# Padded rows for the DRAM tensors and the x tile of layer 0, in a four-layer graph network

## The chip, the cores and the metric

The kernel runs on one core of one Trainium2 chip. The metric is the device time of one execution in microseconds. A core has five engines that run side by side: TensorE (PE, matrix products; its weight loads are listed as PEld), VectorE (DVE), ScalarE (ACT), GpSimd (POOL) and SyncE (SP). Transfers between DRAM and the on-chip memory (SBUF, 128 partitions) are issued by an engine's queue, here nearly all by SP's, and carried out by 16 DMA engines. A transfer consists of runs: stretches of bytes that are contiguous at both ends. The trace records each run as one packet.

## The reference, cut to what matters

The inputs are x (64 graphs, 256 nodes, 256 features) and adj (64 x 256 x 256), all float32. Four layers follow each other, each with a residual and a layer norm. Layer 0 is a recurrence over the 256 nodes, and it is the one that the change is about:

```python
d = jnp.sum(adj, axis=-1)
dinv = jnp.where(d != 0, 1.0 / jnp.where(d != 0, d, 1.0), 0.0)
norm_adjT = jnp.swapaxes(adj, 1, 2) * dinv[:, :, None]

def step(h, i):
    x = jnp.take(h_e, i, axis=1)
    row = jnp.take(norm_adjT, i, axis=1)
    x_par = jnp.einsum('bj,bjd->bd', row, h)          # over all nodes j
    iou = x @ W_ioux.T + b_ioux + x_par @ W_iouh.T + b_iouh
    r, z = jnp.split(iou, 2, axis=1)
    r, z = (jax.nn.sigmoid(r), jax.nn.sigmoid(z))
    hc = jnp.tanh(x @ W_coux.T + b_coux + x_par * r @ W_couh.T + b_couh)
    h_new = z * x_par + (1.0 - z) * hc
    h = jax.lax.dynamic_update_slice(h, h_new[:, None, :], (0, i, 0))
    return (h, None)
```

Node i's step needs the new states of all nodes before it, and the old states (x) of those from i on. Layer 1 is a normalized graph convolution, layer 2 a masked attention with one head, layer 3 a masked attention with eight heads. They work on each graph by itself:

```python
x = _layernorm(x + _L0_gnn_ref(x, adj, ...), axis=-1)
x = _layernorm(x + _L1_gnn_ref(x, adj, ...), axis=-1)
x = _layernorm(x + _L2_gnn_ref(x, adj, ...), axis=-1)
x = _layernorm(x + _L3_gnn_ref(x, adj, ...), axis=-1)
```

## The kernel before, in words

The kernel has a setup, then `_recurrence` (layer 0, all 64 graphs at once, node by node), then `_layers` (layers 1 to 3, a pipeline over graphs). A state of 64 graphs x 256 features lies as 128 partitions x 128 numbers: partition is half of the features times graph.

The sum x_par of a node is put together from parts, by how far back the node j lies:

- From the old states. In the setup, and later beside the steps (`x_side`), PE multiplies adj with x, and `x_out` (L217) stores the products in the DRAM tensor `Us`. `sums_in` (L313) loads the sums of eight nodes at a time as the tile ACC: 128 partitions x 8 nodes x 128 numbers, 512 KB.
- From states long past (`early`). `early_load` (L378) fetches new states from the DRAM tensor `Hd` as the tile Hs (16 to 112 nodes as partitions, eight graphs, 256 features: 8 KB for each partition) and the pieces of adj that go with them as the tile A (runs of 128 bytes). PE multiplies them, and the result is stored in the DRAM tensor `Es` (L430); `early_in_part` (L441) loads it for eight nodes at a time as early_sb, 512 KB.
- From states 9 to some 60 steps back (`late`, L491). They lie in the SBUF ring `Hw`, with the node as the partition. `into_ring` (L652) writes every new state hs into it, in two transfers of 32 KB. PE multiplies ring and adj for the eight nodes of the next block; `send` (L499) stores the result in the DRAM tensor `Lb` and `receive` (L506) loads it back as late_sb, 512 KB. The way through DRAM moves the numbers from one partition layout to the other.
- From the last steps. DVE (`push`, L626) and POOL (`push_far`, L658) add the newest states to ACC directly.

`flush` (L634) copies 32 rows of the ring to `Hd` every 32 steps, in transfers of 8, 16 or 32 partitions with 32 KB each. `load_x` (L564) loads x of eight nodes in two transfers of 256 KB (tile xq). Every tile is transferred by SP's queue.

The order is written out by hand in the loop over n (L757). A block is eight steps, and p = n mod 8. In the steps p < 4, at most two waiting loads a step are issued (`next_load`: Hs, A, S, raw, the x side). The end of a step issues early_sb at p = 0, ACC at p = 1 and xq at p = 2. The states go into the ring at p > 3, two a step. The late products run at p = 0 to 3, their results leave with Lb and come back with late_sb around p = 4 and 5, and POOL adds late_sb to ACC (L876) at p = 6 and 7. At every 32nd step, the tables S, raw and rows of the next 32 nodes are loaded too. All of this goes through one queue in program order, so a transfer that has to wait there holds up all those behind it.

The tiles in DRAM are dense: node, graph and feature lie behind each other. So where a load takes several nodes of one partition, its run is as long as all of them: 4096 bytes for ACC, early_sb and late_sb (8 nodes x 512 bytes), 4096 for xq (4 nodes x 1024), 8192 for Hs (8 graphs x 1024) and 32,768 for the flush (32 graphs x 1024).

Of the kernel before, what the change touches and what calls it, by code (L numbers as in the profile page):

```python
# [9 lines left out]
F32 = mybir.dt.float32  # L10
# [9 lines left out]
P = 128  # L20
# [50 lines left out]
def _recurrence(tc, ident, Hd, x, adj, W_ioux, b_ioux, W_iouh, b_iouh, W_coux, b_coux, W_couh, b_couh, wide, then):  # L71
# [19 lines left out]
    nc = tc.nc  # L91
    B, N, D = x.shape
    T = 32
    NB = N // T
    U = 8
# [4 lines left out]
    NG = B // 4  # L100
# [3 lines left out]
    with ExitStack() as ctx:  # L104
# [85 lines left out]
        for w in range(2):  # L190
            first = (w * T - W + T // 2) % W
# [13 lines left out]
        )  # L205

        dram = ctx.enter_context(tc.tile_pool(name="r_dram", bufs=2, space=bass.MemoryType.DRAM))
        Us = dram.tile([2, B, N, P], F32, name="Us", bufs=1)

        def x_product(pb, at, A, Xs):  # L210

# [42 lines left out]
        def copy_later(out, in_, then=None):  # L254
            def f(n):
                nc.scalar.copy(out, in_)
                held.pop(0)
                if then:
                    then(n)

            copies.append(f)

        def load_later(out, in_, rank):

            begun = []

            def f(n):
                with nc.allow_non_contiguous_dma(reason="bias vector across partitions"):
                    nc.sync.dma_start(out, in_)
                begun.append(n)  # L270

            loads.append((rank, f))
            loads.sort(key=lambda e: e[0])
            return begun
# [5 lines left out]
        def at_step(n, f):  # L280
            transfers.setdefault(n, []).append(f)
# [3 lines left out]
        def base_bank(shape, name):  # L285

            while len(held) == 3:
                next_of(copies, now)
            held.append(name)
            return ps.tile(shape, F32, tag="base", name=name, bufs=3)  # L290
# [85 lines left out]
        Es = {}  # L376

        def early_load(e, got=[]):  # L378

            _, k, lo, hi, t = early.pop(e)  # L380
            rows = hi - lo
            if t == 0:
                Es[k, lo] = dram.tile([2, NG, 4, T, P], F32, name=f"Es_{k}_{lo}", bufs=1)
            Hs = wide.tile([P, GB, D], F32, tag="wide", name=f"Hs_{k}_{lo}_{t}")
            last = [load_later(
                Hs[0:rows], Hd[lo:hi, t * GB:(t + 1) * GB, :], 1
            )]
            if t % 2 == 0:
                A = stream.tile([P, 2 * GB, T], F32, tag="A", name=f"A_{k}_{lo}_{t}")
                last.append(load_later(  # L390
                    A[0:rows],
                    adj[t * GB:(t + 2) * GB, lo:hi, k * T:(k + 1) * T].rearrange("b j i -> j b i"), 1
                ))
                got[:] = [A]
            early_in.append((last, k, lo, hi, t, Hs, *got))

        def early_ahead(n):
            ready = [e for e, piece in enumerate(early) if piece[0] <= n]
            if len(early_in) < 4 and ready:

                half = [e for e in ready if early[e][4] % 2 and early[e - 1:e] != [
                    early[e][0:4] + (early[e][4] - 1,)
                ]]
                early_load((half + ready)[0])
# [86 lines left out]
        def late(first):  # L491

            k, i = divmod(first, T)
            An = tables[k]["An"]
            lb = stream.tile([P, NG, D], F32, tag="lb", name=f"lb_{first}", bufs=1)
            Lb = dram.tile([2, NG, 4, U, P], F32, tag="Lb", name=f"Lb_{first}")
            sides[first] = blk.tile([P, U, P], F32, tag="late", name=f"late_sb_{first}", bufs=1)

            def send():  # L499
                for c in range(2):  # L500
                    nc.sync.dma_start(
                        Lb[c].rearrange("n q u f -> (q u) n f"),
                        lb[i // U::T // U, :, c * P:(c + 1) * P],
                    )

            def receive():  # L506
                nc.sync.dma_start(sides[first], Lb.rearrange("c n q u f -> (c n q) u f"))

            def then(n):
                at_step(n, send)  # L510
                at_step(n + 1, receive)

            n = yield
            for u in range(0, NG // 2, 2):
                pb = [base_bank([P, 2, D], f"late_{first}_{u}_{g}") for g in range(2)]
                for e in range(2):
                    for q in range(4):
                        for g in range(2):
                            rows = slice(g * W, (g + 1) * W)
                            b = (u + e) * 4 + q  # L520
                            nc.tensor.matmul(  # L521
                                pb[g][q * T:(q + 1) * T, e, :],
                                An[rows, b].rearrange("p u s -> p (u s)"),
                                Hw[rows, b, :], start=True, stop=True,
                            )
                    if e:
                        for g in range(2):
                            at = g * NG // 2 + u
                            copy_later(
                                lb[:, at:at + 2, :], pb[g],  # L530
                                then if g and u + 2 == NG // 2 else None,
                            )
                    n = yield
# [29 lines left out]

        def load_x(a):  # L564

            xq = stream.tile([P, U // 2, D], F32, tag="xq", name=f"xq_{a}")
            for h in range(2):
                at = a * U + h * U // 2
                nc.sync.dma_start(xq[h * B:(h + 1) * B], x[:, at:at + U // 2, :])
            return xq  # L570

        def flip_x(a, e, xq):
# [138 lines left out]
        stream = ctx.enter_context(tc.tile_pool(name="r_stream", bufs=2))  # L711
# [3 lines left out]
        tables[0]["Sd"] = chain_S(0)  # L715
        tables[0]["An"] = late_load(0)
        xq = {a: load_x(a) for a in range(2)}
        for a in range(3):
            sums_in(a)
# [37 lines left out]
        for now in range(N):  # L757
            n = now
            k, i = divmod(n, T)
# [24 lines left out]
            if p == 0 and U < n + U < N:  # L784
                late_side = late(n + U)
                next(late_side)
# [98 lines left out]
            if p == 2 and n // U + 2 < N // U:  # L885
                xq[n // U + 2] = load_x(n // U + 2)
# [404 lines left out]
def _load_layers(nc, wide, load, w1, b1, l2, l3):  # L1291

    t1, t2, t3 = (wide.tile([P, 8, 256], F32, tag="wide", name=f"weights_{l}") for l in (1, 2, 3))
    nat = t1[:, 0:2]
    load(nat, w1.rearrange("(c p) d -> p c d", p=P))
    W = []
    for t, l in ((t2, l2), (t3, l3)):
        W.append({})  # L1300
        for s, n in enumerate("qkvo"):
            W[-1][n] = t[:, 2 * s:2 * s + 2]
            load(W[-1][n], l["W" + n].rearrange("(k p) n -> p k n", p=P))
    rows = [t1[:, 2 + s] for s in range(3)]
    for r, b in zip(rows, (b1, l2["bo"], l3["bo"])):
        load(r, b.unsqueeze(0).to_broadcast([P, 256]))
    cols = t1[:, 5, 0:12].rearrange("p (s c) -> p s c", c=2)
    for s, b in enumerate((l2["bq"], l2["bk"], l3["bq"], l3["bk"], l3["bv"], l2["bv"])):
        load(cols[:, s, :], b.rearrange("(c p) -> p c", p=P))
    return nat, *W, *rows, cols  # L1310
# [111 lines left out]
@with_exitstack  # L1422
def kernel(ctx: ExitStack, tc: tile.TileContext, ins, out):
    nc = tc.nc
    x, adj = ins["x"], ins["adj"]
    B, N, D = x.shape
    main = ctx.enter_context(tc.tile_pool(name="main", bufs=1))
    dram = ctx.enter_context(tc.tile_pool(name="dram", bufs=1, space=bass.MemoryType.DRAM))
    ident = main.tile([P, P], F32, name="ident")
    make_identity(nc, ident)  # L1430
    Hd = dram.tile([N, B, D], F32, name="Hd")
    l2, l3 = (
        {w + n: ins[f"{l}_gnn_{w}{n}"] for w in "Wb" for n in "vkqo"} for l in ("L2", "L3")
    )
    wide = ctx.enter_context(tc.tile_pool(name="wide", bufs=4))
    weights = []

    def load_layers(load):
        weights.extend(
            _load_layers(nc, wide, load, ins["L1_gnn_W"], ins["L1_gnn_b"], l2, l3)  # L1440
        )

    _recurrence(
        tc, ident, Hd, x, adj,
        *(ins["L0_gnn_" + n] for n in (
            "W_ioux", "b_ioux", "W_iouh", "b_iouh", "W_coux", "b_coux", "W_couh", "b_couh"
        )),
        wide, load_layers,
    )
    Yd = dram.tile([B, P, 2, D], F32, name="Yd")  # L1450
    found = _layers(tc, ident, Hd, Yd, x, adj, weights, out)
    with tc.If(found > 0):
        _layer_3(tc, ident, Yd, adj, l3, out)
# [36 lines left out]
```

## Time and profile before

| What | Before |
|---|---|
| median of 3 runs | 3354.61 us (3352.26 to 3360.83) |
| profiled execution, time and span | 3353.51 us, 3351.7 us |
| mean granted clock of PE | 0.976 |
| PE, DVE, ACT, POOL busy | 3131.6, 2554.5, 1838.6, 1845.0 us |
| DMA packets, bytes | 528,608, 364.62 MB |
| packets on SP's queue | 510,520 |
| setup, before the first step | 138 us |
| recurrence, 256 steps | 138 to 1472 us |
| layers 1 to 3 | from about 1480 us to the end |

The rows come from the page of the profile, the last three from the trace's start times. A page's busy share is a mean over stages that are limited by different things, so the stages have to be read apart: the slices of the page and the windows (busy time of each engine in a stretch, followed by the granted clock, the busy share of the DMA engines and the GB/s that they moved) do that. The list of waits gives, for an engine and a line, what ended its idle time, with the total in us, the number of times and the longest. The chain of waits is the chain of work that ended last, as start, length, and what it was. In a timeline, SPq is SP's queue issuing a transfer; its duration is the time for which the queue was held by the issue, and not that of the transfer.

### The profile page before, as it was taken

To read this page: it belongs to the slowest core of one execution; us is meant where nothing else is said; L and a number is where in the kernel's file an instruction comes from. 1 tells how busy PE (TensorE), PEld (TensorE's weight loads), DVE (VectorE), ACT (ScalarE), POOL (GpSimd) and SP (SyncE) were. 2 spreads that over 40 slices of the span, in tenths; PEclk is the share of its full clock that TensorE was granted. 3 is DMA by queue.
4 is the path that set the end of the run, shared out by engine and by line. 5 is a ranking of instruction groups with operands and counts; after the bars stand their busy time and mean duration, and the time that the engine had idled before them with its cause. 6 is when DMAs were issued, how large, how long until landed. Compare 5 with 4: busy or idle time off the path is not lost.

```text
span 3351.7 us, 78940 instructions
## 1 busy us (share of the span) xinstructions
PE 3131.6 (93%) x28584; PEld 2311.5 (69%) x28584; DVE 2554.5 (76%) x7381; ACT 1838.6 (55%) x4754; POOL 1845.0 (55%) x2165
## 2 busy tenths in 40 slices
PE   5799998998879998969999999999999999999997
PEld 4566665555545555547888888888888888888885
DVE  3487777776667878856888888888888888888885
ACT  0155554544445544535666666666666666666664
POOL 2377777766667878833444444444444444444443
PEclk7899999999999999989999999999999999999999
DMA  9856685788877675241221211122222222222210
GB/s 292 247 161 156 168 194 152 179 198 207 204 181 178 163 174 152 65 105 47 56 57 54 57 56 54 54 55 58 57 58 58 58 57 58 57 58 58 58 33 20
DMA packets 528608, 364.62 MB, mean 109 GB/s; under 512 B 246620, under 2 KB 494568, under 8 KB 522984
## 3 DMA queue, kind: packets, MB, share of 16 engines
q1 hardware_dynamic: 510520, 342.63, 39.6%
q10 hardware_dynamic: 17696, 16.91, 1.5%
q8 instruction: 229, 3.75, 0.5%
q14 instruction: 163, 1.34, 0.1%
HBM read 240.78 MB, written 99.61 MB: 102 GB/s over the span
## 4 chain that ended last, share of the span: by engine, by line
PE 77%; DMA 8%; DVE 7%; issue 2%; SPq 2%; ACT 2%; POOL 1%; DVEq 0%; ACTq 0%; POOLq 0%
PE mm L997 14%; PE rc L605 6%; PE rc L597 4%; PE s L1195 4%; PE mm_2f L997 3%; PE mm_3v L997 3%; PE mm_3f L997 3%; PE mm_2v L997 3%; PE late L521 3%; PE mm_t L997 3%; PE mm_2s L997 3%; PE mm_g L997 3%; PE mm_2w L997 3%; PE o L1230 3%; DVE ACC L630 3%; PE o L1221 3%
## 5 line engine op out<-in xcount | busy, mean ns | idle before, releaser
L1207 POOL TENSOR_TENSOR p3s<-p 128x256 f32<-128x256 f32 x512 | 358.9, 733 | 364.7 <-ACT p L1205 364.6
L630 DVE SCALAR_TENSOR_TENSOR ACC<-keep,S,ACC 128x128 f32<-128x128 f32 x1712 | 479.1, 343 | 16.9 <-POOL ACC L876 11.2
L997 PE MATMUL mm<-xT,weights 128*128 128x256 f32 x2048 | 483.7, 384 | 2.7 <-ACT xT L1094 2.7
L997 PEld LDWEIGHTS mm<-xT,weights 128*128 128x128 f32 x2048 | 386.0, 191 | 79.9 <-issue 25.5
L1204 DVE TENSOR_TENSOR p<-s,neg 128x512 f32<-128x512 f32 x512 | 317.6, 682 | 118.2 <-PE s L1195 118.2
L667 POOL TENSOR_TENSOR ACC<-ACC,far 128x384 f32<-128x384 f32 (+1 forms) x313 | 372.1, 1189 | 24.5
L663 POOL TENSOR_TENSOR far<-hs,S 128x384 f32<-128x384 f32 (+1 forms) x313 | 304.7, 973 | 4.7
L1205 ACT ACTIVATE p<-p 128x512 f32<-128x512 f32 x512 | 292.4, 626 | 1.6 <-DVE p L1204 1.6
L961 ACT ACTIVATE y<-y,shift,rstd 128x256 f32<-128x256 f32 x512 | 272.9, 599 | 26.6 <-DVE shift L959 22.7
L597 PE MATMUL rc<-WxT,xqT 128*64 128x256 f32 x2048 | 274.8, 390 | 1.1 <-issue 1.1
L1119 ACT ACTIVATE qk<-mm,weights 128x256 f32<-128x256 f32 x256 | 107.5, 471 | 301.9 <-PE mm L997 301.9
L805 POOL TENSOR_TENSOR ready<-ACC,dinv 128x128 f32<-128x128 f32 x255 | 102.1, 400 | 304.7 <-DVE ACC L630 304.2
L1108 POOL TENSOR_TENSOR y<-y,g 128x512 f32<-128x512 f32 x64 | 81.0, 1266 | 301.8 <-issue 301.8
L1244 DVE RECIPROCAL rT<-o 128x256 f32<-128x256 f32 x128 | 223.7, 1748 | 0.3 <-PE o L1221 0.2
L949 DVE BATCH_NORM_STATS2 st<-y 128x6 f32<-128x256 f32 x512 | 209.6, 409 | 13.1 <-POOL y L1108 10.3
L521 PE MATMUL late<-Hw,An 64*32 64x256 f32 x3840 | 166.7, 400 | 42.1 <-DMA Hw<-hs 18.8
L605 PE MATMUL rc<-WhT,rT 128*64 128x128 f32 x2048 | 172.5, 290 | 35.6 <-DVE rT L828 33.2
L824 ACT ACTIVATE rs<-rc 128x128 f32<-128x128 f32 x256 | 71.1, 278 | 245.0 <-PE rc L605 245.0
L605 PEld LDWEIGHTS rc<-WhT,rT 128*64 128x64 f32 x2048 | 109.1, 138 | 133.2 <-DVE rT L828 110.8
L953 POOL TENSOR_TENSOR rstd<-rstd,mhalf 128x2 f32<-128x2 f32 x256 | 173.8, 697 | 47.9 <-DVE rstd L952 34.6
L1066 POOL TENSOR_TENSOR dis<-dis,mhalf 128x2 f32<-128x2 f32 x64 | 44.9, 702 | 273.2 <-DVE dis L1065 261.8
L605 PE MATMUL rc<-WhT,xpT 128*64 128x128 f32 x2048 | 169.4, 286 | 18.1 <-ACT xpT L614 18.1
(162 smaller groups left out, 7255.4 us busy)
## 6 DMA issues: line engine op xcount, KB each, us to landing
xX<-in_x_dram ACTq DMA_DIRECT2D x16, 1024.0 KB
Us<-xu SPq DMA_DIRECT2D x64, 256.0 KB
xq<-in_x_dram SPq DMA_DIRECT2D x64, 256.0 KB
ACC<-Us SPq DMA_DIRECT2D x32, 512.0 KB
Es<-eu SPq DMA_DIRECT2D x64, 256.0 KB
early_sb<-Es SPq DMA_DIRECT2D x32, 512.0 KB
xin<-in_x_dram SPq DMA_DIRECT2D x64, 256.0 KB
ad<-in_adj_dram SPq DMA_DIRECT2D x64, 256.0 KB
```

The costliest lines, as they stand in the source:

```text
L521: nc.tensor.matmul(pb[g][q * T:(q + 1) * T, e, :], An[rows, b].rearrange("p u s -> p (u s)"), Hw[rows, b, :], start=True, stop=True,)
L597: nc.tensor.matmul(G[o * B:(o + 1) * B], xqT[a, i // 2][:, i % 2, kc, h * B:(h + 1) * B], WxT[:, kc, o, gates], start=False, stop=False, s ...
L605: nc.tensor.matmul(G[o * B:(o + 1) * B], hT[:, kc * B:(kc + 1) * B], WhT[:, kc, o, g], start=False, stop=(kc == 1), skip_group_check=True,)
L630: nc.vector.scalar_tensor_tensor(acc[:, 0, :], keep[:, j % 2, :], s, acc[:, 0, :], ALU.mult, ALU.add)
L663: nc.gpsimd.tensor_mul(tmp[:, 0:count, :], hs.unsqueeze(1).to_broadcast(shape), s.unsqueeze(2).to_broadcast(shape),)
L667: nc.gpsimd.tensor_add(acc, acc, tmp[:, 0:count, :])
L961: nc.scalar.activation(y[:, c, :], y[:, c, :], AF.Identity, bias=shift[:, c:c + 1], scale=rstd[:, c:c + 1],)
L997: nc.tensor.matmul(pm[:, c, :], lhsT[:, k, c * P:(c + 1) * P], rhs[:, k, :], start=(k == 0), stop=(k == 1),)
L1204: nc.vector.tensor_add(p, s_ps[i], self.neg3)
L1205: nc.scalar.activation(p, p, AF.Exp, scale=ISQ)
L1207: nc.gpsimd.tensor_add(both, p[:, 0, :], p[:, 1, :])
L1244: nc.vector.reciprocal(rT, o_ps[:, 1, :])
```

## The change

Five DRAM tensors or groups of them and one SBUF tile get longer rows, of which only the first part is used. `Us`, every `Es` and every `Lb` get rows of 128 + 64 numbers, of which 128 are used; `Hd` gets rows of 256 + 64; the SBUF tile xq gets 256 + 4. Every instruction and every transfer is the same as before in number, order and bytes. But a load over several rows is no longer contiguous at both ends, so it goes in runs of one row: 512 bytes for ACC, early_sb and late_sb, 1024 bytes for Hs, for the flush and for xq.

```diff
-        Us = dram.tile([2, B, N, P], F32, name="Us", bufs=1)
+        Us = dram.tile([2, B, N, P + 64], F32, name="Us", bufs=1)[..., 0:P]
...
-                Es[k, lo] = dram.tile([2, NG, 4, T, P], F32, name=f"Es_{k}_{lo}", bufs=1)
+                Es[k, lo] = dram.tile(
+                [2, NG, 4, T, P + 64], F32, name=f"Es_{k}_{lo}", bufs=1
+            )[..., 0:P]
...
-            Lb = dram.tile([2, NG, 4, U, P], F32, tag="Lb", name=f"Lb_{first}")
+            Lb = dram.tile([2, NG, 4, U, P + 64], F32, tag="Lb", name=f"Lb_{first}")[..., 0:P]
...
-            xq = stream.tile([P, U // 2, D], F32, tag="xq", name=f"xq_{a}")
+            xq = stream.tile([P, U // 2, D + 4], F32, tag="xq", name=f"xq_{a}")
...
-                nc.sync.dma_start(xq[h * B:(h + 1) * B], x[:, at:at + U // 2, :])
+                nc.sync.dma_start(xq[h * B:(h + 1) * B, :, 0:D], x[:, at:at + U // 2, :])
...
-    Hd = dram.tile([N, B, D], F32, name="Hd")
+    Hd = dram.tile([N, B, D + 64], F32, name="Hd")[:, :, 0:D]
```

## The prediction

> **What bounds the kernel now.** I read the page's slices first, then the chain of waits, the list of waits, SP's timeline and the windows. The slices show two halves:
>
> ```profile
> DMA  9856685788877675241221211122222222222210
> GB/s 292 247 161 156 168 194 152 179 198 207 204 181 178 163 174 152 65 105 47 56 57 54 57 56 54 54 55 58 57 58 58 58 57 58 57 58 58 58 33 20
> DMA packets 528608, 364.62 MB, mean 109 GB/s; under 512 B 246620, under 2 KB 494568, under 8 KB 522984
> ```
>
> From slice 18 on (1480 us) the layers run with the DMA engines 20% busy and PE busy for 1830 of 1860 us. Of the padded tensors only y<-Hd is read there, and that load already goes in runs of 1024 bytes, since one graph's rows lie apart. I count those 1880 us as untouched. What can move is the recurrence, 138 to 1472 us. The start times of the product rT (L828) put its 256 steps at 5.2 us on average, and eight calm steps at 37.5 to 40.5 us. The blocks of eight that begin at 499, 665, 755, 800, 847, 942 and 993 us take 47.7, 49.9, 45.4, 47.4, 53.4, 51.3 and 48.4. That is some 65 us over calm in seven blocks, and the chain of waits names DMA in them:
>
> ```profile
> 786.37 7.92 DMA Lb<-lb
> ...
> 798.64 4.17 DMA Hw<-hs
> ...
> 803.91 5.43 DMA Hw<-hs
> 809.69 0.67 PE late L521 x16
> ...
> 841.28 3.78 DMA late_sb<-Lb
> ```
>
> The reader should see the order: a store of the sides to DRAM that lands late, copies of the state queued behind its read-back, then PE's late products waiting. The list of waits agrees:
>
> ```profile
> PE late L521 <- DMA Hw<-hs: 18.8, 7, 5.6
> POOL ACC L876 <- DMA late_sb<-Lb: 13.7, 4, 6.2
> PE late L521 <- DMA Hs<-Hd: 5.5, 2, 4.7
> ```
>
> These transfers are late because one queue, SP's, carries everything in order. Its timeline in such a block:
>
> ```profile
> 804.71 0.60 SPq L269 DMA_DIRECT2D Hs<-Hd  x1
> 805.40 0.37 SPq L269 DMA_DIRECT2D A<-in_adj_dram  x1
> 805.87 6.21 SPq L430 DMA_DIRECT2D Es<-eu  x2
> 812.12 1.31 SPq L447 DMA_DIRECT2D early_sb<-Es  x1
> ...
> 816.93 11.55 SPq L269 DMA_DIRECT2D Hs<-Hd  x1
> ...
> 831.16 5.75 SPq L269 DMA_DIRECT2D raw<-in_adj_dram  x1
> 837.01 1.31 SPq L501 DMA_DIRECT2D Lb<-lb  x2
> ```
>
> An issue normally takes 0.3 to 0.7 us. These long ones stand where too much is still in the queue. By the trace's issue and packet records, two things stop SP:[...] about 2000 runs in flight (the two Es of 512 runs each stand behind A with 1792 runs of 128 bytes; raw stands behind S with 2624). So the number of runs matters by itself, and the change raises it.
>
> [...] The rows[...] (busy time by engine, then clock, DMA share, GB/s):
>
> ```profile
> 849.00:850.00 1.00, 1.00 (x14) 0.75 (x11) 0.90 (x4) 0.40 (x1) 0.92 (x2) 1.00 1.13 340
> 137.00:139.00 2.00, 1.91 (x16) 1.31 (x13) 0.42 (x1) 0.11 (x1) 2.00 (x3) 0.61 1.02 418
> 819.00:825.00 6.00, 5.89 (x97) 3.30 (x93) 5.51 (x19) 3.43 (x11) 2.68 (x3) 1.00 1.00 253
> 649.00:651.00 2.00, 2.00 (x33) 1.15 (x25) 1.97 (x9) 0.94 (x5) 1.07 (x2) 1.00 1.02 169
> 653.00:655.00 2.00, 2.00 (x27) 1.13 (x23) 1.93 (x9) 0.27 (x1) 1.80 (x3) 1.00 0.57 87
> ```
>
> Row one is Es and Hw in 512-byte runs, row two ACC in 4096-byte runs over 128 partitions, row three mostly Hs in 8192-byte runs over 112 partitions, row four mostly xq in 4096-byte runs over 64. [...]418 against 340 for the run length, and 169 for 64 partitions although the runs are long. The packet records say the same: a 32 KB run of Hd<-Hw takes 2.0 us at the median with 32 rows, 2.7 with 16 and 4.7 with 8; an 8 KB run of Hs takes 0.50 with 112 rows and 0.61 with 64. I go by both: what makes Hs slow is mostly the partitions, which the change leaves alone.
>
> **The change, part by part.** Bytes stay at 364.62 MB. Stores to Us, Es and Lb and the last Hd<-hs have 512-byte rows already: nothing. What is cut:
>
> 1. ACC<-Us (32), early_sb<-Es (32), late_sb<-Lb (30): 128 runs of 4096 bytes become 1024 of 512. 524 KB at 418 GB/s is 1.25 us, at 340 it is 1.54: +0.3 each, 28 us of DMA time in all. A trace reason for less: when several loads overlap, the 4096-byte runs take 0.22 us on average and not the 0.16 of a calm one, so part is lost today already (bound 0).
> 2. Hs<-Hd (64 transfers, 4608 runs of 8192 bytes become 36,864 of 1024). A 1024-byte packet over 128 partitions takes 0.046 us in the records, so 356 GB/s over 16 engines. The 112-row load, 917 KB, is 3.6 us at 253 and 2.6 at 356: at best -1.0. For 64 rows and fewer[...] 0. I take a third of the best for the 32 loads of 112 and 80 rows, -0.4 each, -12 us of DMA time. Bounds: 0, and -42 if every Hs (37.7 MB) went at 356.
> 3. Hd<-Hw (24; 496 runs of 32 KB become 15,872 of 1024) and xq (64; 64 runs of 4096 become 256 of 1024, its rows now at a pitch of 1040 bytes):[...] 0. Bounds -10 and +10 us of DMA time.
> 4. The queue. Packets grow by 84,224 + 32,256 + 15,376 + 12,288 = 144,144. Hs of 112 rows, with 112 runs today, fits beside A's 1792 under the 2000; with 896 it does not, nor does ACC's 1024 beside A's 1280, nor two loads of 1024 beside each other. The next one is then let in only when the one ahead is done, and the engines run dry between. What that costs is seen between S and raw, 653 to 655 us: a share of 0.57 over 2 us, 0.86 us idle. With 32 A loads and a hundred loads of 896 or 1024 runs I count about 24 such gaps in the busy blocks (300 to 1000 us): +21 us of idle DMA. Bounds: 0, if more is admitted than I think, and 100, if each of some 110 pairs pays.
>
> What of this reaches the end? Between 300 and 1000 us the DMA share is 0.7 to 0.8, and about half of its blocks (7 of some 17) show a stall that ends on DMA; where they do not, the next p<4 stage absorbs the delay. I take half for what falls there. Part 1: two thirds of 28 falls in these blocks, half is +9. Part 2: half of -12 is -6. Part 4: half of +21 is +10. Sum +13 us. Before 138 us the setup is DMA-bound, but its stores and loads are not cut; the first ACC load, which DVE waits for 12.5 us, is 0.3 longer. I neglect it. The cover for the rest is PE, DVE and POOL work of the steps; were it gone everywhere, parts 1, 2 and 4 would cost 37 us.
>
> The sum stands against the profiled run's own 3353.5 us (span 3351.7): 3366.5. The median of the runs is 1.1 above that run, so 3367.
>
> **Rivals.**
>
> Faster: short runs flow better. If Hs goes at 356 GB/s and the flush gains too, the backlog ahead of Lb (three Hs of 896 KB stand there at 816 us) lands 3 us sooner, in about eight blocks: -24, so 3331. For it: 253 GB/s at a DMA share of 1.00 is far below 418[...]. Against it: xq is slow too with runs half as long, and follows the row count. It decides once Hs falls by over 0.8 us a load with fewer gaps than 10.
>
> Hidden: the DMA work changes by a few us a block and the steps cover it, 3355. For it: blocks 21 to 31 (after 1040 us) have a share of 0.4 to 0.67 and, but for the one that begins at 1199 us, no stall to speak of. Against it: seven blocks have no slack.
>
> Much slower: every pair of 1024-run loads pays a gap, SP is held longer, and Lb, late_sb and the copies of hs, which follow in the same queue, are late in 12 to 15 blocks by 4 to 5 us: +60, 3415. Against it: loads of 512 and 1024 runs kept the DMA share at 0.96 before 138 us, though ACT's queue helped there.
>
> No effect: the runs are merged anyway and packets stay at 528,608: 3355.
>
> **How the numbers follow.** A run of this kernel can't tell less than 0.3%, 10 us, from no change (its three runs span 8.6). Chances: forecast (+10 to +40) 0.40, faster 0.26, hidden 0.20, much slower 0.10, no effect 0.04. So slower 0.50, same 0.24, faster 0.26. The range leaves out the far half of the faster case and the upper half of the much slower one: 3332 to 3405. The forecast's own range is 3364 to 3394.
>
> **What would show it.** Right: about 672,750 packets and the same bytes; a window with ACC loads alone at 340 GB/s and not 418; Hs of 64 rows as slow as now; more time in SP's issues of A, ACC and Hs; longer blocks among those named, and the layers at the same length. Wrong: Hs windows at 320 GB/s or more, a shorter Lb or Hw<-hs on the chain, or stalls of SP that shrink because fewer bytes stand in the queue.

## The result, and the profile after

The changed kernel takes 3386.78 us (median of 4 runs, 3385.11 to 3392.17), the kernel before 3353.44 beside it: a ratio of 1.0099, with a 95% interval of 1.0079 to 1.0118, so +33 us where +13 was forecast. The page of the changed kernel, its span, the slices of the DMA engines, the packets and SP's queue (packets, MB, share of 16 engines' span):

```profile
span 3383.4 us, 78940 instructions
...
DMA  9856686788787575331222222222222222222210
...
DMA packets 672752, 364.62 MB, mean 108 GB/s; under 512 B 246620, under 2 KB 659944, under 8 KB 672232
...
q1 hardware_dynamic: 654664, 342.63, 41.0%
```

The bytes are the same and there are 144,144 packets more, as counted ahead. The starts of rT, from its first to its last, give the stages: setup +0.7 us, recurrence from 1330.6 to 1361.0, +30.4, and all that follows from 1879.9 to 1880.6. So nearly all of the loss lies in the recurrence. The list of waits names who is late (total in us, times, longest), here for 140 to 1480 us; the line numbers are two higher than before, as the change adds two lines:

```profile
POOL ACC L878 <- DMA late_sb<-Lb: 34.8, 9, 6.9
...
PE late L523 <- DMA Hw<-hs: 22.7, 7, 4.9
...
POOL An L481 <- DMA raw<-in_adj_dram: 16.0, 2, 9.7
...
PE late L523 <- DMA A<-in_adj_dram: 9.4, 2, 5.6
```

POOL waited 13.7 us in 4 places for late_sb before, and now 34.8 in 9. The chain of waits (start, length) shows the same order as before, in more blocks: the side's store, its read-back, then a copy of the state.

```profile
666.07 3.65 DMA Lb<-lb
669.80 5.21 DMA late_sb<-Lb
...
681.04 5.08 DMA Hw<-hs
...
802.05 6.88 DMA Lb<-lb
...
809.06 4.15 DMA late_sb<-Lb
...
819.17 5.37 DMA Hw<-hs
...
1004.96 6.93 DMA Lb<-lb
...
1011.96 4.31 DMA late_sb<-Lb
```

In the recurrence, late_sb stands on that chain 8 times with 35.7 us, against 3 times with 10.2 before.

The run length shows where the forecast looked for it. This is the window with ACC loads alone:

```profile
137.00:139.00 2.00, 1.65 (x12) 0.90 (x8) 0.38 (x1) 0.00 (x0) 1.49 (x3) 0.50 1.15 347
```

347 GB/s in 512-byte runs, where 4096-byte runs had 418. So the mechanism of part 1 is there; the experiments ask what the rest of the 33 us is.

### The profile page after: what moved, and what is told of

Its sections match the earlier page's. It is cut to its first block, busy times and chain, and to the rows that moved or that the text cites. A ratio compares the mean times of both kernels' runs of the same rounds, so it can differ in the third digit from the quotient of the medians.

```text
span 3383.4 us, 78940 instructions
## 1 busy us (share of the span) xinstructions
PE 3138.8 (93%) x28584; PEld 2316.1 (68%) x28584; DVE 2553.4 (75%) x7381; ACT 1838.8 (54%) x4754; POOL 1842.8 (54%) x2165
## 3 DMA queue, kind: packets, MB, share of 16 engines
q8 instruction: 229, 3.75, 0.5%
## 4 chain that ended last, share of the span: by engine, by line
PE 76%; DMA 8%; DVE 8%; issue 2%; ACT 2%; SPq 2%; POOL 1%; DVEq 0%; POOLq 0%; ACTq 0%
PE mm L999 14%; PE rc L607 6%; PE rc L599 4%; PE s L1197 4%; PE mm_2f L999 3%; PE mm_3v L999 3%; DVE ACC L632 3%; PE late L523 3%; PE mm_3f L999 3%; PE mm_2v L999 3%; PE mm_t L999 3%; PE mm_2s L999 3%; PE mm_g L999 3%; PE mm_2w L999 3%; PE o L1232 3%; PE o L1223 2%
## 5 line engine op out<-in xcount | busy, mean ns | idle before, releaser
L951 DVE BATCH_NORM_STATS2 st<-y 128x6 f32<-128x256 f32 x512 | 209.6, 409 | 13.0 <-POOL y L1110 10.2
```

## Experiments

All times below are differences to the kernel before, run in the same set on the same chip, and worked out as (ratio - 1) x 3355 us. Single changes of 4 to 7 us are close to what the intervals (about 4 us either way) can tell.

### Which part costs: one edit at a time

The rates come first. A stretch behind the last layer was added to the kernel before: some 235 us of loads of x and adj into tiles of their own, with nothing else running. Nothing was left out.

```diff
+            (long,) * 6, (short,) * 6, (hs_long,) * 4, (hs_short,) * 4,
+            (few_long,) * 4, (few_short,) * 4,
+            (hs_long, cut) * 3, (hs_short, cut) * 3, (long, cut) * 3, (short, cut) * 3,
```

Here long and short are 512 KB over 128 partitions in runs of 4096 and 512 bytes; hs is 112 partitions in runs of 8192 and 1024; few is the same with 64; cut is a load in 128-byte runs like A's, 1792 of them.

> The kernel before, with loads added behind the last layer, when nothing else uses the DMA engines: six loads of 512 KB to 128 partitions in runs of 4096 bytes, six in runs of 512; four of 112 rows of 8 KB in one run each and four in runs of 1024; the same with 64 rows; and alternating pairs with a load of 1792 runs of 128 bytes. The added time itself says nothing. Run-length theory (part 1 of the forecast): about 415 GB/s for the 4096-byte runs, 340 for the 512-byte ones. [...]the 64-row loads pace alike with both run lengths, near 200 GB/s; the 112-row loads differ by under 10%. Its rival: the 112-row loads reach 330 GB/s or more in runs of 1024 and stay under 280 in runs of 8192. Queue theory (part 4): a load of 896 or 1024 runs in front of one of 1792 leaves the engines idle for about 0.9 us between them, a load of 112 or 128 runs leaves no gap. If neither pair shows a gap, part 4 falls.

Windows in the steady part of each group, in the order long, short, hs_long, hs_short, few_long, few_short, hs_long with cut, hs_short with cut (the last three numbers are clock, DMA share and GB/s):

```profile
3470.00:3473.00 3.00, 0.00 (x0) 0.00 (x0) 0.29 (x2) 0.00 (x0) 0.00 (x0) 0.50 1.02 400
3479.00:3484.00 5.00, 0.00 (x0) 0.00 (x0) 0.58 (x4) 0.00 (x0) 0.00 (x0) 0.50 1.20 290
3490.00:3497.00 7.00, 0.00 (x0) 0.00 (x0) 0.44 (x3) 0.00 (x0) 0.00 (x0) 0.50 1.00 286
3503.00:3510.00 7.00, 0.00 (x0) 0.00 (x0) 0.29 (x2) 0.00 (x0) 0.00 (x0) 0.50 1.11 284
3516.00:3521.00 5.00, 0.00 (x0) 0.00 (x0) 0.29 (x2) 0.00 (x0) 0.00 (x0) 0.50 1.02 210
3527.00:3532.00 5.00, 0.00 (x0) 0.00 (x0) 0.29 (x2) 0.00 (x0) 0.00 (x0) 0.50 1.13 205
3534.00:3546.00 12.00, 0.00 (x0) 0.00 (x0) 0.73 (x5) 0.00 (x0) 0.00 (x0) 0.50 1.05 244
3547.00:3561.00 14.00, 0.00 (x0) 0.00 (x0) 0.88 (x6) 0.00 (x0) 0.00 (x0) 0.50 1.07 236
```

Three readings. Runs of 512 bytes back to back drop to 290 GB/s. The pattern of Hs gains nothing from short runs, with 112 partitions (286 and 284) or with 64 (210 and 205), where the forecast had -0.4 us a load for 80 and 112. And the pair with A's runs keeps the DMA share at 1.07: the gap of 0.86 us that part 4 took from the stretch between S and raw is not there, but for one dip of about half a microsecond (a share of 0.85 over 3550 to 3553 us), at the first pair of the row, which SP issued after a wait. The pairs of 512-byte runs with A's, not shown, have a share of 0.93 over 3570 to 3581 us; it is 0.36 from 3573.5 to 3575.5, again where SP had waited, and 1.12 from there to 3581. So a gap at every pair is not seen.

Then the change was taken apart. Each of these kernels has some lines of the change and leaves the others as before: only Lb; only Hd; only Us and Es; the whole again; the x tile alone; and the four DRAM edits without the x tile.

```diff
+            Lb = dram.tile([2, NG, 4, U, P + 64], F32, tag="Lb", name=f"Lb_{first}")[..., 0:P]
...
+    Hd = dram.tile([N, B, D + 64], F32, name="Hd")[:, :, 0:D]
...
+        Us = dram.tile([2, B, N, P + 64], F32, name="Us", bufs=1)[..., 0:P]
```

> Only the sides Lb have padded rows, so that only the 30 loads late_sb<-Lb go in runs of 512 bytes. My forecast's sum gives this part a third of part 1 and little of part 4: +3 to +5 us. The rival that the trace after suggests (POOL's wait for late_sb grew from 13.7 us in 4 waits to 34.8 in 9): this read-back has no slack, because POOL waits for it at p = 6 and 7 and the copies of the state stand behind it in the queue: +12 to +20 us, more than half of the whole loss.

> Only the states Hd have padded rows: Hs loads and the flush in runs of 1024 bytes. Queue theory: A with up to 1792 runs can no longer share the queue with Hs, +8 to +15 us. Faster-flow rival: Hs and flush land sooner, -5 to -15 us. Read-back rival: within 4 us of before.

> Only Us and Es have padded rows: the 64 loads of ACC and early_sb in runs of 512 bytes. Forecast: two thirds of part 1 and the pairs with A and with each other of part 4, +8 to +12 us. Read-back rival: these loads are issued 8 to 16 steps ahead of their use, so 0 to +4 us.

> The changed kernel once more, beside the kernels below on one chip. The three parts run alone lost 6.4, 7.0 and 4.4 us by their ratios, 18 in sum. If the parts add up and xq costs nothing, this is +18; if they don't (each takes the slack that another would need) or if xq costs, it is +28 to +36, as when it was first measured.

> Only the tile xq is padded, to a pitch of 1040 bytes. Forecast (part 3): 0, within 3 us. Rival: a pitch[...] makes each run slower (its packets rose from 73 ns a KB to 84), +5 to +15 us.

> The changed kernel with the tile xq dense as before. If xq costs nothing, the same as the changed kernel; if the pitch of 1040 bytes is what was overlooked, 8 to 15 us less; it is +18 if the three other parts simply add.

| Kernel | Ratio, 95% interval | us |
|---|---|---|
| only Lb: late_sb in 512 | 1.0019, 1.0008 to 1.0031 | +6.4 |
| only Us and Es: ACC and early_sb in 512 | 1.0013, 1.0002 to 1.0024 | +4.4 |
| only Hd: Hs and the flush in 1024 | 1.0021, 1.0012 to 1.0031 | +7.0 |
| these three together | 1.0044, 1.0027 to 1.0060 | +14.8 |
| only the x tile's rows | 1.0045, 1.0029 to 1.0062 | +15.1 |
| the whole change again | 1.0079, 1.0063 to 1.0096 | +26.5 |

The parts add up, within their intervals: the three DRAM parts to 17.8 where 14.8 was measured, and 14.8 and 15.1 to 29.9 where the whole has 26.5 here and 33 in the first set. But the x tile, taken as free, costs as much as the other three together. A second stretch of added loads asks whether its rate is the reason: x over twice 64 partitions, at a pitch of 1024, 1040 and 1280 bytes, and 128 partitions in runs of 4096, 2048, 1024 and 512.

```diff
+                (runs_4096,) * 6, (runs_2048,) * 6, (runs_1024,) * 6, (runs_512,) * 6,
+                (half(D),) * 6, (half(D + 4),) * 6, (half(D + 64),) * 6,
```

> The kernel before with loads added behind the last layer: 512 KB to 128 partitions in runs of 4096, 2048, 1024 and 512 bytes, six each; the xq pattern (two halves of 64 partitions) with a pitch of 1024, 1040 and 1280 bytes; and single loads of 512 KB with runs of 4096 and of 512 bytes, each waited for. Run-length theory: about 400, 380, 345 and 290 GB/s (the first and the last as the first series gave them). Alignment theory: the xq pattern is 10% or more slower at 1040 than at 1280[...]. A single load takes 0.5 to 0.8 us longer from issue to use in runs of 512.

It measured 394, 358, 362 and 290 GB/s for the four run lengths over 128 partitions, and 393 for 2048 bytes, 339 for 1024 and 290 for 512 in a second turn, so that only the shortest runs stand clearly apart in both. A single load that is waited for takes 3.25 to 3.47 us from its issue to VectorE's use of it in runs of 4096 bytes and 3.56 to 3.75 in runs of 512: 0.3 longer, as the forecast had it, and not 0.5 to 0.8. The windows of the x pattern, with dense rows, rows at 1040 and rows at 1280 bytes:

```profile
3399.00:3405.00 6.00, 0.00 (x0) 0.00 (x0) 0.37 (x3) 0.00 (x0) 0.00 (x0) 0.50 1.03 235
3412.00:3422.00 10.00, 0.00 (x0) 0.00 (x0) 0.61 (x4) 0.00 (x0) 0.00 (x0) 0.50 1.13 222
3427.00:3434.00 7.00, 0.00 (x0) 0.00 (x0) 0.46 (x3) 0.00 (x0) 0.00 (x0) 0.50 1.12 235
```

235, 222 and 235 GB/s; a second turn of the same loads gave 248, 229 and 232. Six per cent on 64 loads of 1.1 us (256 KB at 235 GB/s) is an estimated 4 us of DMA time, and not 15 us of the kernel's. That speaks against the rate but does not exclude it: inside the kernel the padded x tile's packets take 11 to 14 us more in sum.

### Runs, or places? The x tile without its short runs

The tile xq lies in a pool of SBUF (the stream pool) together with other tiles. Padding it also moves what lies behind it. Two kernels separate that: dense x tiles with 64 bytes behind each (runs as before, neighbours moved by as much as in the change), and two runs of 2048 bytes with 32 bytes between them. The padded x tile was run again with them.

```diff
-            xq = stream.tile([P, U // 2, D], F32, tag="xq", name=f"xq_{a}")
+            xq = stream.tile([P, U // 2 * D + 16], F32, tag="xq", name=f"xq_{a}")[:, 0:U // 2 * D].rearrange("p (u d) -> p u d", d=D)
```

> The x tile's rows at 1040 bytes alone, a second time and beside the two that follow. If its first measurement (+15 us) is a property of the edit, +15 within 6. If it came from that set of executions, whose spread was some 10 us either way, 0 to +5.

> The kernel before with 64 bytes of padding behind each x tile: its rows stay dense, the transfers stay in runs of 4096 bytes, only what lies behind the tile in on-chip memory moves by as much as with the padded rows. Theory of addresses (what costs is that the other tiles moved): +15, like the padded rows. Theory of runs (what costs is the 256 runs in place of 64 in each transfer): 0 within 4. Theory of a kernel so finely timed that any edit disturbs it: anywhere from +4 to +15.

> Each partition's x rows in two runs of 2048 bytes with 32 bytes between, so 128 runs a transfer in place of 64 (and not 256). The loads behind the last layer gave 2048-byte runs about the rate of longer ones. If the number of runs in SP's queue is what costs, a third of what the padded rows cost (+5 within 4, since 64 runs more in place of 192 more); if the padding itself or its odd addresses cost, +15; if only runs of 1024 bytes are slow, 0.

Padded again: 1.0047 (1.0030 to 1.0065), +15.8. Dense with 64 bytes behind: 1.0032 (1.0018 to 1.0047), +10.7. Two runs of 2048: 1.0041 (1.0025 to 1.0057), +13.8. The theory of runs falls: a kernel whose packets are those of the kernel before, to the last one, has most of the loss.

That could still mean that any edit hurts so finely timed a kernel, or that kernels compared in this way come out slower for no reason of their own. Four more: an unchanged copy; one more instruction in the setup; the DRAM tensors as large as in the change but with dense rows, so that only addresses in DRAM move; and 32 bytes behind the dense x tile in place of 64.

```diff
+    nc.vector.tensor_copy(ident[0:1, 0:1], ident[0:1, 0:1])
...
-    Hd = dram.tile([N, B, D], F32, name="Hd")
+    Hd = dram.tile([N * B * (D + 64)], F32, name="Hd")[0:N * B * D].rearrange("(n b d) -> n b d", n=N, b=B)
...
+            xq = stream.tile([P, U // 2 * D + 8], F32, tag="xq", name=f"xq_{a}")[:, 0:U // 2 * D].rearrange("p (u d) -> p u d", d=D)
```

> The kernel before, unchanged. If the intervals mean what they say: a ratio of 1.000 within 0.0015 (0 within 5 us). If kernels that are compared with the kernel before come out slower for a reason that is not in them, +4 to +10 us, and each single part must be read against that.

> The kernel before with one more instruction in the setup: VectorE copies one number of ident onto itself. No address and no transfer changes. Theory of a finely timed kernel that any edit disturbs: +4 to +12. Theories of runs and of addresses: 0 within 4.

> Us, Es, Lb and Hd allocated as large as in the changed kernel, but their rows dense, so runs and queue are those of the kernel before and only addresses in DRAM move. The three DRAM parts together cost +15 with their shorter runs. Theory of runs (94 loads that take 0.5 us longer back to back, half of it on the path): 0 within 4. Theory of addresses: +8 to +15. Theory of any edit: +4 to +12.

> Dense x tiles with 32 bytes behind each in place of 64. Theory of addresses on the chip: +5 to +14 (64 bytes moved it by some 11, and two runs of 2048 bytes with 32 bytes between by 14). Theory of runs: 0 within 4. Theory of any edit: +4 to +12.

| Kernel | Ratio, 95% interval | us |
|---|---|---|
| unchanged copy | 0.9997, 0.9985 to 1.0009 | -1 |
| one more instruction | 0.9998, 0.9986 to 1.0010 | -1 |
| larger DRAM tensors, rows dense | 0.9997, 0.9986 to 1.0009 | -1 |
| 32 bytes behind each x tile | 1.0054, 1.0035 to 1.0072 | +18 |

So the comparison is sound, and neither an edit as such nor these addresses in DRAM cost anything that can be measured: what the three DRAM parts cost is their run length. On the chip it is the other way round: where the neighbours lie costs 11 to 18 us.

### The same x tile, moved out of the way

If that is so, the padded x tile is free where it moves nobody. It was put into a pool of its own, opened behind the two others, so that the tiles behind x in them lie 8192 bytes lower and keep their places modulo 8192: dense, padded, and with the whole change.

```diff
+        last_pool = ctx.enter_context(tc.tile_pool(name="r_last", bufs=2))
...
+            xq = last_pool.tile([P, U // 2, D + 4], F32, tag="xq", name=f"xq_{a}")
```

> The kernel before with the x tile in a pool of its own, opened last, so that the other tiles of the two pools lie 8192 bytes lower and keep their places modulo 8192. Control for the next run. If only the odd 32 or 64 bytes matter: 0 within 5. If any move of the tiles costs: +10 to +18.

> The same with the x tile's rows at 1040 bytes: its transfers go in runs of 1024 bytes, and no other tile moves against the control. If the move of the other tiles was the whole cost of the padded x rows: the control's ratio within 4 us. If the runs cost: the control's +8 to +15.

> The whole change, with its x tile in that last pool. If what is left is the three DRAM parts: +15 within 5, as they cost together. If the runs of the x tile cost too: +26 to +33, as the change as it stands.

Dense 0.9990 (0.9981 to 1.0000), padded 0.9990 (0.9977 to 1.0002), the whole change 1.0051 (1.0036 to 1.0065), +17. The padded x tile, runs of 1024 bytes and all, costs nothing there, although its packets do take longer: their times, summed over a run and spread over 16 engines, are 73.0 us dense and 86.1 padded. Its own second buffer moves by 64 bytes there too, so it is the neighbours that count. The whole change without the moved neighbours costs what its DRAM parts cost, within the intervals: +17 against the kernel before and some +20 against the dense control, which is the fairer measure, as the setup is shorter in the traces of these three kernels (133.8 to 138.7 us, against 139.7 to 141.2 in the kernel before and the three that match it). None of them is clearly faster than the kernel before.

### What a moved neighbour does, in one place

The first place where the traces part is the end of the second block of eight steps. SP sends late_sb, two rows loads and then twelve copies of the state to the ring. First the unchanged copy, in SP's timeline (start, time for which SP is held):

```profile
199.41 0.38 SPq L507 DMA_DIRECT2D late_sb<-Lb  x1
199.90 1.18 SPq L301 DMA_DIRECT2D rows<-in_adj_dram  x2
201.12 11.02 SPq L656 DMA_DIRECT2D Hw<-hs  x12
212.25 0.93 SPq L220 DMA_DIRECT2D Us<-xu  x2
```

The window over the six microseconds in which these transfers run, in the copy:

```profile
200.00:206.00 6.00, 6.00 (x64) 4.46 (x61) 4.73 (x18) 3.06 (x10) 5.70 (x6) 1.00 0.69 189
```

And the list of waits of the copy from 200 to 222 us, where it names the stores and what follows them:

```profile
ACT xu L256 <- DMA Us<-xu: 1.6, 1, 1.6
...
PE rc L605 <- ACT xpT L614: 1.2, 1, 1.2
```

PE's first products behind that wait (in brackets, its length and what ended it), and the window around them:

```profile
217.81 0.66 PE L605 MATMUL rc<-WhT,xpT 128*64 128x128 f32 x8 [1.25 <-ACT xpT L614]
...
217.50:220.90 3.40, 3.00 (x53) 1.93 (x57) 1.50 (x6) 2.00 (x9) 3.17 (x4) 1.00 1.12 349
```

Now the kernel with 64 bytes behind the dense x tile. It is here 1.7 us earlier than the copy, because its setup was that much shorter. SP's timeline:

```profile
197.67 0.40 SPq L507 DMA_DIRECT2D late_sb<-Lb  x1
198.16 1.18 SPq L301 DMA_DIRECT2D rows<-in_adj_dram  x2
199.39 12.40 SPq L656 DMA_DIRECT2D Hw<-hs  x12
211.90 1.38 SPq L220 DMA_DIRECT2D Us<-xu  x2
```

The same window of it, counted from the same step:

```profile
198.30:204.30 6.00, 6.00 (x64) 4.46 (x61) 4.73 (x18) 3.06 (x10) 5.63 (x6) 1.00 0.79 187
```

And its list of waits, from 198 to 222 us:

```profile
ACT xu L256 <- DMA Us<-xu: 3.4, 1, 3.4
...
PE rc L605 <- ACT xpT L614: 3.1, 1, 3.1
```

The same products in it, and their window:

```profile
217.87 1.12 PE L605 MATMUL rc<-WhT,xpT 128*64 128x128 f32 x8 [3.06 <-ACT xpT L614]
...
217.50:220.90 3.40, 3.03 (x33) 1.98 (x33) 0.51 (x3) 1.89 (x8) 2.00 (x2) 0.50 1.13 358
```

About the same bytes (189 and 187 GB/s over 6 us) take the DMA engines 0.79 of the time and not 0.69; a 4096-byte packet there takes 275 ns on average and not 237. So the ring's copies hold SP 1.4 us longer, the stores to Us that follow are late, ACT, which wants to overwrite xu, waits 1.8 us longer, and PE behind it 1.8 (3.06 and not 1.25).

The step is 2.8 us longer, and the last microsecond has another source. After the wait of 3.06 us, PE's clock is granted at 0.50 for 3.4 us, and the same eight products take 1.12 us and not 0.66; after the wait of 1.25 us the clock stays at 1.00. So a stall costs more here than it lasts. Over the whole recurrence the clock stands at 0.50 for 58 to 72 us in the kernel before and the three that match it, for 85 and 99 in the two traces of the changed kernel, and for 61 to 89 in the five with only the x tile edited. The eight products took 1.7 times as long at 0.50. Were it twice for all of PE's work there, half of the 13 to 41 us that the changed kernel spends more at 0.50 would be lost: at most 7 to 20 us of its loss, an estimate from these sums. It follows the waits and is not their cause: at 200 to 206 us both kernels have 1.00.

The engines themselves are not slower. The two traces have the same 78,940 instructions with the same semaphores, and the medians of VectorE's, ScalarE's and GpSimd's lines in the recurrence differ by at most 3 ns.

The place is not a single execution's accident: in the five kernels in which only the x tile is edited in place the share in these 6 us is 0.78 to 0.81 and the step loses 1.3 to 2.8 us; in the kernel before, the one with one more instruction, the one with larger DRAM tensors and the two with the x tile in its own pool, the share is 0.67 to 0.71 and the step differs by -0.03 to +0.5 us. The share alone doesn't make the loss, though: the three DRAM parts together have 0.78 there, with late_sb in 512-byte runs, and this step loses 0.05. Nor does the step need moved tiles to lose: Hd alone has a share of 0.66 and loses 1.1. What happens in the other blocks was not followed step by step.

Why a packet takes longer is not shown. When x is edited in place, the tiles behind it in the stream pool stand 64 or 128 bytes from their old places, and 8192 bytes from them when x has its own pool; no other move was tried. What the records of packets give is uneven:

- In this stretch a 4096-byte packet takes 16% longer (275 and 237 ns), although half of these packets belong to late_sb, which lies in another pool and did not move.
- Stores from the moved tiles xu, eu and lb do take longer, but by little: the 512-byte packets of Us<-xu average 29.2 to 29.5 ns in the five kernels with x edited in place, against 27.9 to 28.1 with the old places. Es<-eu has 29.2 to 29.9 against 28.0 to 28.6, and Lb<-lb 28.7 to 29.1 against 27.7 to 28.0, but 27.7 with 32 bytes behind x.
- The source hs of the ring's copies moves too, and its packets stay nearly as they were: 28.2 to 28.5 ns where the tiles moved by 128 bytes, against 27.9 to 28.4.

The DMA time as a whole says little: up to 1490 us, SP's packets sum to 957 to 970 us in the four kernels with the old runs and places, and to 967 to 976 in the three with moved neighbours and x in runs of 2048 bytes or more.

## Why the prediction was wrong, and where it was right

Direction and the stage were right: slower, in the recurrence alone, through late_sb, the ring's copies and SP. The size was too small by 20 us. The step that failed most is part 3's zero for xq: it was priced by its 64 partitions alone, and the padded tile costs 15 us, because it moves the tiles behind it. The second is part 2: Hs and the flush in short runs were to save 6 us, and cost 7. Part 1 was 2 us too low, and part 4's +10 has no ground that was found. Together, 13 + 15 + 13 + 2 - 10 is 33.

Step by step, with the packet times of each tile summed over the run and spread over 16 engines (packets counted to transfers in the order of issue), four kernels with the runs of before (the kernel itself, the copy, the one with one more instruction, the larger DRAM tensors) against the changed one:

| Tile | Before, us | After, us |
|---|---|---|
| ACC | 54.8 to 56.3 | 68.0 |
| early_sb | 55.3 to 57.4 | 60.0 |
| late_sb | 46.3 to 50.0 | 57.2 |
| Hs and flush together | 231.4 to 233.8 | 247.4 |
| xq | 74.1 to 75.8 | 85.8 |

- Part 1, run length of ACC, early_sb, late_sb: right. +28 us of DMA time was forecast and about +25 came (12, 4 and 9). Half of what falls in the busy blocks on the path, +9: the parts alone gave 4.4 + 6.4 = 10.8. The 290 GB/s of loads back to back, against 400, would have given 0.5 us a load, an estimate, but among the recurrence's other traffic ACC and late_sb pay 0.3 to 0.4, and early_sb 0.1.
- Part 2, Hs: wrong in sign. -12 us of DMA time and -6 on the path were forecast; the packets of Hs and flush take about +15 and the part alone costs +7. "I take a third of the best" for 80 and 112 rows was the failing step: alone, the pattern has one rate at both run lengths, and in the recurrence it is slower with the short one; why, is open. The window of 253 GB/s was not its long runs: with nothing else running 286 and 284 GB/s stand alike. There the rate of long runs went with the partitions: 210 GB/s with 64, 286 with 112, 394 and 400 with 128.
- Part 3, flush and xq, "0": right for the flush to the eye (it can't be told from Hs), and right for xq's runs, whose +11 to +14 us of DMA time is free (padded in its own pool: 0.9990). The step still failed, and this is the largest miss: the pad was taken to touch only the transfer of xq, and what lies behind xq in the pool was not asked. Its neighbours' new places cost 11 to 18 us.
- Part 4, the queue: a gap of 0.86 us is not found in the steady pairs of the added stretch, so "+10" had no such ground. Nor do "about 2000 runs in flight", the author's estimate, come out as a limit: in the recurrence of the kernel before, by the packets counted to transfers, 79 issues would have brought the runs in flight over 2000; 41 of them held SP for more than 1 us and 38 did not, against 111 of the other 1025. It is a tendency. What the change does to SP is to hold its issues longer. From the first rT to the last they hold SP for 950 to 960 us in the four kernels with the old runs, 966 with Lb alone, 989 with Hd alone, 986 with Us and Es, 1021 with all three and 1049 in the whole change. A's 32 issues show it best, here in the three DRAM parts together (least, median and longest, in ns; medians of 418 to 436 and a longest of 667 to 1377 in the four kernels):

```profile
L269 SPq DMA_DIRECT2D A<-in_adj_dram x32: 375/822/6572, 280.3 to 1218.9; - x32
```

  That this is how Hd alone costs 7 us is not shown, and there is a case against it: the padded x tile in its own pool holds SP for 981 us, its dense control for 952, and the two take the same time.
- "I take half for what falls there" roughly held for the DRAM parts, whose 40 us of DMA time cost 15 to 20. It does not hold beside them: the padded x tile's 13 us cost nothing in its own pool, and where its neighbours move, 10 us or less of DMA time cost 11 to 18.
- That these DRAM parts cost 15, near the +13 of the sum, is luck: -6 for Hs and +10 for gaps make +4, both without ground, where Hd costs +7.

The sum of measured terms, 11 for part 1, 7 for Hd and 15 for the moved neighbours, is 33, with some 4 us of doubt in each; the change measured 33 and, again, 26.5. Of the rivals, "faster" falls with Hs's rate, "hidden" with ACC and late_sb, and "no effect" with the packets. "Much slower" had the places right (late_sb waited for in 9 blocks), but not the reason, as no gaps were found. The share of 0.4 to 0.67 that "hidden" cites for the blocks after 1040 us is 0.14 to 0.82 in stretches of 40 us.

What stays open: why places on the chip matter to the DMA engines, whether xu, eu and lb are the tiles that count, and whether all of the 11 to 18 us comes in the way shown for one block.

## What to carry to other kernels

A pad in SBUF is two edits: it changes a transfer's runs, and it moves every tile behind it (here +11 and +18 us with the runs unchanged). Test it with the pad at the end of the last pool, or with a dense tile and the same bytes behind, before its cost is put down to the transfer. Price a run length from a window of the very traffic that the load runs beside, and ask whether the rate changes with the run length at its number of partitions: with 112 it was 286 and 284 GB/s in runs of 8192 and 1024, with 128 it was 400 and 290 in runs of 4096 and 512. Ask what a wait of PE does to its clock: here one of 3.06 us was followed by 3.4 us at 0.50. An unchanged copy in the comparison is cheap and tells which differences of 0.1 to 0.2% may be read at all.

## What the runs showed of the hardware beyond that

- Dense x tiles with 32 or 64 bytes behind, every packet the same in number and size: +18 and +11 us of 3355, and with 64 bytes +16% in the time of a 4096-byte packet in one stretch of 6 us (275 and 237 ns).
- A wait of PE of 3.06 us was followed by 3.4 us at half the granted clock, one of 1.25 us at the same place was not.
- 128 partitions, DRAM to SBUF, loads back to back: 394 and 400 GB/s in runs of 4096 bytes, 358 and 393 in 2048, 362 and 339 in 1024, 290 in 512, the last in three series. A single 512 KB load took 0.3 us longer in runs of 512 than of 4096. 112 partitions 286 and 284 in runs of 8192 and 1024; 64 partitions 210 and 205.
- Rows of x at a pitch of 1040 bytes are 1 to 6% slower than at 1280 (222 and 229 against 235 and 232 GB/s), at the same run length, with nothing else running.
